# Seven-product steps for layers 2 and 3 of neighbouring pairs in a four-layer graph network

## The chip, the cores and the metric

The kernel runs on one core of a Trainium2 chip. The metric is the device time in microseconds, less being better. Arithmetic is in 32-bit floating point, with the masks of layer 1 in bfloat16. Engines are named as in the profile: PE (TensorE: matrix products), DVE (VectorE), ACT (ScalarE), POOL (GpSimd) and SP (SyncE). POOL and SP serve here as queues that issue DMAs.

## The reference, cut to what matters

x has 8 batches of 2048 nodes with 64 features, adj is a 2048x2048 matrix with rows normalised. There are four layers, each followed by `x = layernorm(x + layer(x))` over the 64 features:

```python
# layer 0: Chebyshev graph convolution, K = 3
As = [I, A, 2 A A - I]
out = einsum('bnki,nkio->bno', einsum('knm,bmc->bnkc', As, x), einsum('nd,dkio->nkio', embedding, weight)) + b
# layer 1: attention over all nodes; the mask is adj > 0.5
e = leaky_relu(s1[:, :, None] + s2[:, None, :]); att = softmax(where(mask, e, -9e15)); out = elu(att @ h)
# layer 2
out = (A + I) @ (x W^T + b) / deg
# layer 3, three steps; node 0 is set to a given value first
for _ in range(3):
    v = relu(concat[v, A @ v] W1^T + b1) W2^T + b2
```

So A, or A + I, multiplies the state of all batches twice in layer 0, once in layer 2 and three times in layer 3.

## The kernel before

**Pairs.** Two batches of 64 features make a pair of 128 columns, `NPAIR` = 4 pairs. A pair's state is a tile of [128 nodes, 16 blocks, 128 columns] (`SX[p]`, `SA`, `SB`, `SH`).

**Sweeps.** A product of the matrix with a pair is a `sweep` (L1128). It goes over four column blocks `c` of 512 nodes; in each, 16 matmuls of 128x128 by 128x512 add up in one of two PSUM banks (`acc_ring`). A sweep is 64 such multiplies. `multiply` (L400) splits one by columns into two halves that run side by side, where PE is in that form already. The 2 MiB of a column block come by DMA as eight tiles of 512 KB (`fetch`, L267, on SP's queue, `A_BUFS` = 6 buffers). With `plus`, tiles on the diagonal come from `a_plus_i`, a copy of A + I in HBM, which the first sweep makes. Layer 3's sweeps begin each block with a seed, one more multiply that adds the state times a weight to the bank (`SH_of[p]` by `w31v` in its first step, by `gv` = W2-W1 product later). Evictions (`z_evict`, `h_evict`) hand each finished block to `tails`, which makes the next operand from it: `layer2_tail` and `start_chunk` (embedding, layer norm, transposes), `u_chunk` (the block times W1's second half or `ge`, into `u_of(p, s)`), `last_chunk` (output and `store`).

**Order of the sweeps** (`sweeps`, L1400): layer 0 for all pairs, with layer 2 of pair 0 slipped in; layer 3 of pair 0 (three sweeps); layer 2 of pair 1; layer 3 of pair 1; layer 2 of pairs 2 and 3; at last layer 3 of pairs 2 and 3 together.

**Seven products.** `joint_layer3` (L1225) does that last part. Two pairs are taken as a matrix of two column halves, the nodes as two halves, so that a step is a product of 2x2 blocks, and it uses Strassen's method in Winograd's form: seven block products where eight would be plain. Their left factors are quarters of A and four sums of quarters, `sa` to `sd`, made beforehand in HBM by accumulating DMAs on POOL's queue (`sums_of_a`, L1191); their right factors are sums of u (`sums_of_u`, L1355, on DVE). A step has 7 x 2 x 8 = 112 multiplies and 8 seeds. Each product is done in two passes of 8 multiplies, one for each 512 columns, on the two banks; results are combined on DVE (`x_of`, `z_and_v`, `combine`), one is kept by a copy on ACT (`keep`).

**Layer 1** lies beside the sweeps. Its `scores` (L779) and `weights` (L857, L870) are instructions of [128, 2048] on DVE, its exponentials are ACT's, its products with the state (`po`, L884) PE's, its masks come on POOL's queue (L852, L766). Pair p leaves layer 1 when the token ("x2", p) is set in `finish`; layer 2 of the pair waits for that.

**Plan.** The order of all instructions is written at build time by a list scheduler (`Plan`). Each piece of work is a generator that yields the engine it wants and what it waits for. `Plan.go` always continues the one that can begin first by the planner's costs; a tie goes to the lower rank: 0 for `sums_of_u`, 1 for evictions, 3 for `tails`, 10 to 12 for the later pairs' `weights`, 1000 for the sweeps. `LAG`, `SLACK`, `HOLD` and `BACK` shift the planner's times for it. Some work has a due time: the rows of adj from 130 us on (`rows_of_adj`), the sums of A from 320 us on, one in 14 us.

Of the kernel before, what the change touches and what calls it, by code (L numbers as in the profile page):

```python
# [12 lines left out]
ALU = mybir.AluOpType  # L13
# [24 lines left out]
class Plan:  # L38
# [7 lines left out]
    SLACK = 0.3  # L46
# [5 lines left out]
    HOLD = 0.5  # L52
# [3 lines left out]
        ("add_terms", 0): -0.03,  # L56
        ("add_terms", 1): -0.11,
        ("add_terms", 2): -0.13,
        ("greatest", None): -1.14,
        ("out_of", None): 0.95,  # L60
        ("row_tile", None): -1.44,
        ("scores", 0): -1.14,
        ("start_chunk", None): -0.37,
        ("sums", None): 5.39,
# [111 lines left out]
def resnorm_d4_kernel(  # L176
# [251 lines left out]
    def weights_of_l23():  # L428
# [12 lines left out]

        yield "PE", [pp_ring, yt_ring]
# [28 lines left out]
    def rows_of_adj():  # L471


        for t in range(NT):
            yield "SP", [130.0 + 9.5 * t, bc_ring]
            an, k = bc_ring.take([P, 2, HALF], "an")
            an = an.rearrange("p a b -> p (a b)")
            nc.sync.dma_start(an, adj[t * P : (t + 1) * P, :])
            done = plan.dma("SP", 1024, bc_ring.t, 130.0 + 9.5 * t)
            plan.start(1, row_tile(t, an, k, done))  # L480
# [545 lines left out]
    def layer2_tail(p, c, z, kz, done):  # L1026
# [7 lines left out]
        yt_ring.give(kz, done)  # L1034
# [40 lines left out]
    def u_chunk(p, c, w, dst, bias, s, done):  # L1075

        room = {(0, 0): ["y1 used"], (0, 1): ["w0 used"], (2, 0): [("stored", 0, c)]}.get((p, s), [])
        yield "PE", [done, pp_ring, *room]
# [90 lines left out]
    def refill():  # L1169
        while ahead[0] < len(order_of_a) and a_ring.ready() < NEVER:  # L1170
            if spent[0] < AQ - 2 and ahead[0] > spent[0] + 3:
                break
            fetch(ahead[0])
            ahead[0] += 1
# [15 lines left out]

    def sums_of_a():  # L1191
        n = itertools.count()
        for m, a, b in (
# [5 lines left out]
            for x in (a, b):  # L1199
                for k, r in sum_tiles[m]:  # L1200
                    if x in QUARTER:
                        part = tile_of_adj(k + QUARTER[x][0], r + QUARTER[x][1])
                    else:
                        part = sum_tiles[x][k, r]
                    before = [("sum", m, k, r)] if x == b else []
                    if x not in QUARTER:
                        before.append(("sum", x, k, r, True))
                    yield "DMA", [320.0 + 14.0 * next(n), *before]
                    nc.gpsimd.dma_start(
                        sum_tiles[m][k, r], part, **({"accum_op": ALU.add} if x == b else {})  # L1210
                    )
# [3 lines left out]
    def order_of_joint():  # L1215
        for s in range(3):
            for m in ("sb", "a11", "sc", "sd", "a21", "a22", "sa"):
                for k in range(2):
                    for r in range(RQ):
                        if m in QUARTER:  # L1220
                            order_of_a.append((k + QUARTER[m][0], r + QUARTER[m][1], False))
                        else:
                            order_of_a.append((m, (k, r), False))

    def joint_layer3():  # L1225
        p, o = JOINT
# [4 lines left out]
        X, Z, V = buf[0:3]  # L1231
        T1, T3, T7 = (t.rearrange("p (t n) -> p t n", n=P) for t in buf[3:6])

        for s in range(3):
            up, uo = u_of(p, s), u_of(o, s)
            B11, B21, B12, B22 = up[:, 0:8], up[:, 8:16], uo[:, 0:8], uo[:, 8:16]
            T4, T6 = B21, B12
            plan.start(0, sums_of_u(s, B11, B21, B12, B22, T1, T3, T7))
            seed = gv if s else w31v
            half = lambda t, k: t[:, k * CW : (k + 1) * CW]  # L1240
            banks = {}

            def seeded(pair, c, pa, start):
                nc.tensor.matmul(  # L1244
                    pa,
                    lhsT=seed,
                    rhs=SH_of[pair][:, tiles(c), :],
                    start=start,
                    stop=False,
                    skip_group_check=True,  # L1250
                )
                plan.run("PE", mm(CW))

            def quarter(pa, B, need, start):
                for r in range(RQ):
                    n = next(used)
                    yield "PE", [("a", n), need(r // 2)]
                    at_, kt = a_tiles.pop(n)
                    for b in range(2):
                        nc.tensor.matmul(  # L1260
                            pa,
                            lhsT=B[:, 2 * r + b, :],
                            rhs=at_[:, b, :],
                            start=(start and r == 0 and b == 0),
                            stop=(r == RQ - 1 and b == 1),
                            skip_group_check=True,
                        )
                    done = plan.run("PE", mm(CW, 2), ("a", n), need(r // 2))
                    a_ring.give(kt, done)
                    spent[0] += 1  # L1270
                    refill()
                return done

            def keep(s, k, pa, done):
                yield "ACT", [done]
                nc.scalar.copy(half(X, k), pa)
                at["m5", s, k] = plan.run("ACT", act(CW), done)

            def x_of(s, k, pa, ka, done):
                yield "DVE", [done, ("m5", s, k)]  # L1280
                nc.vector.tensor_tensor(half(X, k), pa, half(X, k), ALU.subtract)
                at["x", s, k] = done = plan.run("DVE", dve(CW), done)
                acc_ring.give(ka, done)

            def z_and_v(s, k, pa, ka, done):
                yield "DVE", [done, ("x", s, k)]
                nc.vector.tensor_tensor(half(Z, k), half(X, k), pa, ALU.subtract)
                at["z", s, k] = done = plan.run("DVE", dve(CW), done)
                yield "PE", [done]
                seeded(p, 2 + k, pa, False)  # L1290
                done = plan.free["PE"] + plan.LAG
                yield "DVE", [done]
                nc.vector.tensor_tensor(half(V, k), pa, half(X, k), ALU.subtract)
                at["v", s, k] = done = plan.run("DVE", dve(CW), done)
                acc_ring.give(ka, done)

            def combine(s, k, what, pair, c, pa, ka, done):

                token = {"c11": "x", "c22": "z", "c21": "v"}[what]
                yield "DVE", [done, sq_ring, (token, s, k)]  # L1300
                tmp, kq = sq_ring.take([P, CW], "c")
                a = half({"x": X, "z": Z, "v": V}[token], k)
                nc.vector.tensor_tensor(
                    tmp, a, pa, ALU.subtract if what == "c21" else ALU.add
                )
                done = plan.run("DVE", dve(CW), done)
                if what == "c21":
                    at["c21", s, k] = done
                else:
                    acc_ring.give(ka, done)  # L1310
                yield from h_evict(pair, s, c, tmp, None, done)
                sq_ring.give(kq, plan.free["ACT"])

            u = lambda pair, side: lambda k: ("u", pair, s, 2 * side + k)
            t = lambda i: lambda k: ("t", s, i, k)
            for k in range(2):
                yield "PE", [acc_ring, u(o, 1)(0)]
                pa, ka = banks[k] = acc_ring.take([P, CW], "acc")
                done = yield from quarter(pa, B22, u(o, 1), True)
                plan.start(1, keep(s, k, pa, done))  # L1320
            for k in range(2):
                yield "PE", [("m5", s, k), ("h", o, s - 1, k)]
                pa, ka = banks[k]
                seeded(o, k, pa, False)
                done = yield from quarter(pa, T3, t(3), False)
                plan.start(1, h_evict(o, s, k, pa, ka, done))
            for k in range(2):
                yield "PE", [acc_ring, t(1)(0)]
                pa, ka = acc_ring.take([P, CW], "acc")
                done = yield from quarter(pa, T1, t(1), True)  # L1330
                plan.start(1, x_of(s, k, pa, ka, done))
            for k in range(2):
                yield "PE", [acc_ring, ("h", p, s - 1, 2 + k)]
                pa, ka = acc_ring.take([P, CW], "acc")
                done = yield from quarter(pa, B11, u(p, 0), True)
                plan.start(1, z_and_v(s, k, pa, ka, done))
            for k in range(2):
                yield "PE", [acc_ring, t(6)(0), ("h", o, s - 1, 2 + k)]
                pa, ka = acc_ring.take([P, CW], "acc")
# [140 lines left out]
```

## Time and profile before

| | us |
|---|---|
| median of three runs (lowest to highest) | 2085.89 (2083.27 to 2085.94) |
| profiled execution | 2081.43 |
| its span, from first to last instruction | 2079.5 |
| PE busy | 2042.8 (98%) |
| DVE busy | 1441.2 (69%) |
| ACT busy | 981.1 (47%) |
| POOL busy | 267.2 (13%) |

The mean granted clock of PE was 0.995 of full speed. The DMAs moved 531.18 MB. Landmarks of the span: the first sweep ends at 130 us; layer 1's weights run from 430 to 1600; the third step of layer 3 for pair 0 follows the eviction at 1187; layer 2 of pair 1 is evicted from 1290 to 1352; the third step of layer 3 for pair 1 follows the eviction at 1517; layer 2 of pair 2 is evicted from 1623 to 1672, that of pair 3 from 1688 to 1736; then come the three joint steps, the last store being issued at 2075. The sums of A are issued from 319 to 1211.

In the rows of the profile an instruction's duration is from its start to its modelled end; matmuls overlap, so the distance between starts tells PE's rate and the mean duration does not. A 32-bit multiply leaves two records.

### The profile page before, as it was taken

Reading aid. Unit: us, or ns where it says so; the run is one execution under the profiler, and the core shown is the slowest. Engines: PE = TensorE matmul, PEld = TensorE weight load, DVE = VectorE, ACT = ScalarE, POOL = GpSimd, SP = SyncE. Lnnn points to the kernel's source line nnn. Section 1 sums busy time; section 2 is a strip of 40 time slices with the busy share of each in tenths; the row PEclk is TensorE's granted clock in tenths of the full one; section 3 lists DMA queues with packets and bytes.
Section 4 is the critical chain, followed back from the end, with each engine's and each line's share of the span. In section 5 each row is a group of like instructions: output and inputs, shape, how many; then the busy total and the mean of one; then the engine's idle time right before and its main releaser. Section 6 shows DMA issues by size and latency. Waiting matters only on the chain.

```text
span 2079.5 us, 22115 instructions
## 1 busy us (share of the span) xinstructions
PE 2042.8 (98%) x7845; PEld 889.4 (43%) x7845; DVE 1441.2 (69%) x1847; ACT 981.1 (47%) x1791; POOL 267.2 (13%) x424
## 2 busy tenths in 40 slices
PE   8999999999999999999999999999999999999997
PEld 3444444444343443444344343443333455444444
DVE  2217566998899999979999979999798422121224
ACT  0015443378887567667766538427567211000002
POOL 2310001221111221021111111010000000000000
PEclk9999999999999999999999999999999999999999
DMA  9889867766546688688769999798787788888885
GB/s 299 290 311 330 306 202 242 279 177 158 141 147 223 164 278 300 221 273 253 251 224 282 287 313 328 255 331 280 243 278 233 256 262 265 266 265 271 263 285 186
DMA packets 223936, 531.18 MB, mean 255 GB/s; under 512 B 21506, under 2 KB 29826, under 8 KB 219458
## 3 DMA queue, kind: packets, MB, share of 16 engines
q1 hardware_dynamic: 170738, 360.73, 51.5%
q0 software_dynamic: 48864, 166.95, 26.4%
q10 hardware_dynamic: 4224, 2.10, 0.4%
q8 instruction: 62, 1.02, 0.2%
q14 instruction: 48, 0.39, 0.1%
HBM read 497.00 MB, written 64.16 MB: 270 GB/s over the span
## 4 chain that ended last, share of the span: by engine, by line
PE 86%; issue 5%; DMA 4%; DVE 3%; ACT 1%; SPq 0%; POOL 0%; POOLq 0%; DVEq 0%; ACTq 0%
PE acc L405 45%; PE yp L655 14%; PE acc L1260 10%; PE po L884 10%; DMA a<-in_adj_t 3%; PE ps_u L405 2%; DVE junk L779 1%; DVE terms L691 1%; PE acc L1244 1%; PE ps_emb L405 1%; PE pf L405 1%; ACT terms L679 1%; PE ps_sv L405 1%; ACT e L865 0%; DVE e L857 0%
## 5 line engine op out<-in xcount | busy, mean ns | idle before, releaser
L405 PE MATMUL acc<-a,SX 128*128 128x512 f32 (+1 forms) x1544 | 521.4, 596 | 7.9 <-DMA SX<-in_x 6.6
L405 PE MATMUL acc<-a,SB 128*128 128x512 f32 (+1 forms) x1000 | 354.7, 598 | 6.5 <-DMA a<-in_adj_t 5.8
L405 PEld LDWEIGHTS acc<-a,SX 128*128 128x128 f32 (+1 forms) x1544 | 196.5, 164 | 281.5 <-issue 270.3
L865 ACT ACTIVATE e<-e,sv 128x1024 f32<-128x1024 f32 x256 | 280.5, 1152 | 75.5 <-DVE e L857 75.1
L679 ACT ACTIVATE terms<-yp,emb_sb 128x128 f32<-128x128 f32 x896 | 242.4, 394 | 133.8 <-PE yp L655 133.4
L857 DVE TENSOR_TENSOR e<-s1b,mk 128x2048 f32<-128x2048 f32 x128 | 289.5, 2286 | 8.7 <-ACT e L865 4.7
L870 DVE TENSOR_TENSOR e<-e,mb 128x2048 f32<-128x2048 f32 x128 | 290.0, 2285 | 6.3 <-ACT e L865 6.1
L779 DVE CUSTOM_DVE_ANT_0 junk<-s2b,mr 128x2048 bf16<-128x2048 f32 x128 | 292.9, 2288 | 2.0
L873 ACT ACTIVATE e<-e 128x2048 f32<-128x2048 f32 x128 | 245.3, 1926 | 69.4 <-DVE e L870 69.1
L884 PE MATMUL po<-e,SX 128*64 128x512 f32 x1024 | 231.6, 595 | 0.0
L405 PEld LDWEIGHTS acc<-a,SB 128*128 128x128 f32 (+1 forms) x1000 | 130.5, 166 | 189.8 <-issue 176.4
L691 DVE TENSOR_TENSOR terms<-terms 128x512 f32<-128x512 f32 (+1 forms) x176 | 130.0, 739 | 27.6 <-ACT terms L679 23.4
L655 PE MATMUL yp<-SH,xgT 64*128 64x512 f32 x512 | 138.5, 618 | 5.6 <-ACT terms L679 4.8
L852 POOL DMA_DIRECT2D mk<-by_col x128 | 72.7, 587 | 526.4 <-DVE e L857 427.6
L655 PE MATMUL yp<-wk,xgT 64*128 64x512 f32 x512 | 132.0, 592 | 0.0
L884 PEld LDWEIGHTS po<-e,SX 128*64 128x64 f32 x1024 | 70.6, 137 | 143.3 <-issue 133.9
L655 PE MATMUL yp<-SH,y2T 64*128 64x512 f32 x512 | 131.2, 589 | 0.0
L405 PE MATMUL acc<-a,SA 128*128 128x512 f32 (+1 forms) x288 | 119.0, 597 | 2.7 <-DMA a<-in_adj_t 2.7
L1260 PE MATMUL acc<-a,t 128*128 128x512 f32 x192 | 85.4, 592 | 0.0
L655 PEld LDWEIGHTS yp<-SH,xgT 64*128 64x128 f32 x512 | 44.5, 187 | 79.2 <-issue 64.9
L655 PEld LDWEIGHTS yp<-wk,xgT 64*128 64x128 f32 x512 | 49.9, 188 | 60.8 <-issue 60.6
L655 PEld LDWEIGHTS yp<-SH,y2T 64*128 64x128 f32 x512 | 49.8, 188 | 60.7 <-issue 60.7
(239 smaller groups left out, 1784.8 us busy)
## 6 DMA issues: line engine op xcount, KB each, us to landing
a<-in_adj_t SPq DMA_DIRECT2D x520, 512.0 KB, 5.9
mr<-by_row POOLq DMA_DIRECT2D x64, 512.0 KB, 6.3
mk<-by_col POOLq DMA_DIRECT2D x128, 256.0 KB, 6.0
an<-in_adj SPq DMA_DIRECT2D x16, 1024.0 KB, 10.4
a<-a_plus_i SPq DMA_DIRECT2D x32, 512.0 KB, 4.4
a<-sb SPq DMA_DIRECT2D x24, 512.0 KB, 4.4
a<-sc SPq DMA_DIRECT2D x24, 512.0 KB, 4.4
a<-sd SPq DMA_DIRECT2D x24, 512.0 KB, 4.6
```

The lines of the kernel that those rows point to most:

```text
L405: nc.tensor.matmul(out[h], lhsT=lhsT[:, h], rhs=rhs, skip_group_check=True, **kw)
L655: nc.tensor.matmul(yp[:, e, :], lhsT=v[rows, cs], rhs=w[rows, hs], start=(k3 == 0), stop=(k3 == 2),)
L679: nc.scalar.activation(batches(terms[0][:, dd, :]), term, AF.Copy, scale=weight)
L691: nc.vector.tensor_tensor(a, a, b, ALU.add)
L779: nc.vector.tensor_tensor_reduce(out=junk, in0=s2b[e][0], in1=masks[t][0], scale=1.0, scalar=LOWEST, op0=ALU.add, op1=ALU.max, accum_out=m ...
L852: nc.gpsimd.dma_start(mk, by_col[jt // 2][:, jt % 2, h * HALF : (h + 1) * HALF])
L857: nc.vector.tensor_tensor(e, s1b[0], mk.unsqueeze(1).to_broadcast([P, 2, HALF]), ALU.add)
L865: nc.scalar.activation(e[:, i, :], e[:, i, :], AF.Prelu, bias=sv[:, 2 + i, jt : jt + 1], alpha=ALPHA)
L870: nc.vector.tensor_tensor(e, e, mb[0], ALU.add)
L873: nc.scalar.activation(e, e, AF.Exp)
L884: nc.tensor.matmul(po[i * C : (i + 1) * C, f, :], lhsT=SX[p][:, t, i * C : (i + 1) * C], rhs=e[:, i, f * CW : (f + 1) * CW], start=(t == 0 ...
L1260: nc.tensor.matmul(pa, lhsT=B[:, 2 * r + b, :], rhs=at_[:, b, :], start=(start and r == 0 and b == 0), stop=(r == RQ - 1 and b == 1), skip ...
```

## The change

The seven-product step is made a function of its own, `joint_step(p, sp, o, s, ...)`, which does step `sp` of pair p together with step `s` of layer 3 of pair o; with `sp` None it does layer 2 of pair p instead, without seeds for it, and its results go to `layer2_tail`. `joint_layer3` calls it three times as before. New is `joined(p)`, called for p = 1 and p = 2 in place of two sweeps: layer 3's third step of pair p-1 and layer 2 of pair p in one seven-product step. Its buffers are `wk1` and the two tiles of `xg_ring`, which layer 0 has left; two of its sums of u take the place of operands that are used up, so those sums wait (for `m5`, for `c22`).

As layer 2 multiplies by A + I, the shared sums and quarters are made of A + I, and layer 3 must use it too: `w31v` becomes W1's first half less its second. In `joint_step` the multiplies go through `multiply`, so that they can take the column form. The sums of A are due from 420 us on, one in 8 us, each as two DMAs of half the size; a tile of a sum isn't fetched before the plan has its sum. `u_chunk` of pair 1 waits for the whole of its joined step. The planner's `SLACK`, `HOLD`, `BACK` and the due times of the rows of adj are changed.

```diff
-    SLACK = 0.3
+    SLACK = 0.0
...
-    HOLD = 0.5
+    HOLD = 0.0
...
     BACK = {
-        ("add_terms", 0): -0.03,
-        ("add_terms", 1): -0.11,
-        ("add_terms", 2): -0.13,
-        ("greatest", None): -1.14,
-        ("out_of", None): 0.95,
-        ("row_tile", None): -1.44,
-        ("scores", 0): -1.14,
-        ("start_chunk", None): -0.37,
-        ("sums", None): 5.39,
+        ("h_evict", None): 0.64,
+        ("keep", None): -0.94,
+        ("layer1", None): -0.21,
+        ("mask_of_tile", None): 5.38,
+        ("tails", None): -0.13,
     }
...
+        nc.vector.tensor_tensor(w31v, w31v, w31e, ALU.subtract)
...
-            yield "SP", [130.0 + 9.5 * t, bc_ring]
+            yield "SP", [115.0 + 9.0 * t, bc_ring]
...
+        if s == 0 and p == 1 and p in JOINED:
+            room = [("joined", p)]
...
+            m, at_, _ = order_of_a[ahead[0]]
+            if isinstance(m, str) and ("sum", m, *at_, True) not in at:
+                break
...
+    SUMS = 420.0
...
-                        part = tile_of_adj(k + QUARTER[x][0], r + QUARTER[x][1])
+                        c, q = k + QUARTER[x][0], r + QUARTER[x][1]
+                        part = a_plus_i[q] if c == q // 2 else tile_of_adj(c, q)
...
-                    yield "DMA", [320.0 + 14.0 * next(n), *before]
-                    nc.gpsimd.dma_start(
-                        sum_tiles[m][k, r], part, **({"accum_op": ALU.add} if x == b else {})
-                    )
+                    yield "DMA", [SUMS + 8.0 * next(n), *before]
+                    for i in range(2):
+                        nc.gpsimd.dma_start(
+                            sum_tiles[m][k, r][:, i, :],
+                            part[:, i, :],
+                            **({"accum_op": ALU.add} if x == b else {}),
+                        )
...
+    def joint_step(p, sp, o, s, bufs, sums):
+
+        X, Z, V = bufs
+        up, uo = SX[p] if sp is None else u_of(p, sp), u_of(o, s)
+        B11, B21, B12, B22 = up[:, 0:8], up[:, 8:16], uo[:, 0:8], uo[:, 8:16]
+        T1, T3, T7, T4 = sums
+        T6 = B12
+        tag = (p, o, s)
...
+            yield "DVE", [done, ("x", tag, k)]
+            nc.vector.tensor_tensor(half(Z, k), half(X, k), pa, ALU.subtract)
+            at["z", tag, k] = done = plan.run("DVE", dve(CW), done)
+            if sp is not None:
                 yield "PE", [done]
                 seeded(p, 2 + k, pa, False)
                 done = plan.free["PE"] + plan.LAG
...
+            if pair == p and sp is None:
+                queue2.append(lambda: layer2_tail(p, c, tmp, kq, done, sq_ring))
+                at["q2", len(queue2)] = done
+                return
...
+        for k in range(2):
+            yield "PE", [
+                ("c21", tag, k),
+                t(4)(0),
+                *([("h", p, sp - 1, k)] if sp is not None else []),
+            ]
...
+    JOINED = (1, 2)
+    room_of_joined = []
+
+    def joined(p):
+        if not room_of_joined:
+            yield "PE", ["w0 used", ("x2", p)]
+            assert xg_ring.ready(2) < NEVER
+            for i in range(2):
+                t, _ = xg_ring.take([P, 2, CW], "ut")
+                room_of_joined.append(t.rearrange("p a n -> p (a n)"))
+        R1, R2 = room_of_joined
+        T3, T1 = (t.rearrange("p (t n) -> p t n", n=P) for t in (R1, R2))
+        B22 = u_of(p - 1, 2)[:, 8:16]
+        yield from joint_step(p, None, p - 1, 2, (wk1, R2, R1), (T1, T3, B22, T1))
+        at["joined", p] = 0.0
...
-            if p:
-                yield from sweep(layer2_product(p))
-            for s in range(3):
+            for s in range(2):
                 yield from sweep(layer3_product(p, s))
-        yield from sweep(layer2_product(NPAIR - 2))
+            if p + 1 in JOINED:
+                yield from joined(p + 1)
+            else:
+                yield from sweep(layer3_product(p, 2))
+                yield from sweep(layer2_product(p + 1))
```

The order of a joined step's products is that of a joint step: m5 and then the sum with T3 on the same banks (pair p-1's blocks 0 and 1), T1, B11, T6 (pair p-1's blocks 2 and 3), T7 (pair p's blocks 2 and 3) and T4 on T7's banks (pair p's blocks 0 and 1).

## The prediction

> **What bounds the kernel now.** I read the page's first two parts first: is there an engine with no time to spare, and where in the span.
>
> ```profile
> span 2079.5 us, 22115 instructions
> PE 2042.8 (98%) x7845; PEld 889.4 (43%) x7845; DVE 1441.2 (69%) x1847; ACT 981.1 (47%) x1791; POOL 267.2 (13%) x424
> ...
> PE   8999999999999999999999999999999999999997
> ...
> DVE  2217566998899999979999979999798422121224
> ```
>
> PE has 36.7 us of idle time in all, so work taken from PE is worth its full price unless something becomes late. The second row is the one to fear: from slice 8 to slice 31 (400 to 1620 us) DVE is nearly as full as PE, by layer 1; after that it is idle and PE works alone.
>
> The groups by shape price the work:
>
> ```profile
> L870 DVE TENSOR_TENSOR e<-e,mb 128x2048 f32<-128x2048 f32 x128 | 290.0, 2285 | 6.3 <-ACT e L865 6.1
> ...
> L1303 DVE TENSOR_TENSOR c<-u,acc 128x512 f32<-128x512 f32 x12 | 8.3, 688 | 40.0 <-PE acc L1260 40.0
> ```
>
> The chain of waits in order of time gives PE's true rate, from a stretch of one joint step where nothing interrupts:
>
> ```profile
> 1880.85 20.60 PE acc L1260 x48
> ```
>
> That is 0.429 us a record. One multiply of 128x128 by 128x512 leaves two records (four of half the price where it is split by columns), so it costs 0.858 us. The stage table shows that a joint step already runs without a gap (110.0 of 110 us busy), and how much room DVE has in the stages where the change puts new ones (columns: us, then busy us of PE, PEld, DVE):
>
> ```profile
> 1187.00:1355.00 168.00, 167.00 (x804) 73.23 (x801) 150.24 (x177) 90.45 (x115) 21.22 (x37) 1.00 0.88 297
> 1355.00:1517.00 162.00, 156.53 (x653) 63.15 (x653) 140.05 (x121) 78.19 (x75) 18.58 (x34) 0.98 0.83 287
> 1517.00:1672.00 155.00, 155.00 (x779) 64.34 (x776) 111.91 (x139) 86.24 (x109) 10.02 (x17) 1.00 0.77 251
> 1760.00:1870.00 110.00, 110.00 (x305) 52.66 (x304) 19.90 (x30) 6.67 (x11) 0.00 (x0) 1.00 0.81 268
> ```
>
> The timelines of DVE and ACT show the handover that matters. Pair 3 leaves layer 1 with its last normalisation, and PE turns to layer 2 of pair 3 when the last column block of pair 2 is evicted:
>
> ```profile
> 1639.84 0.69 DVE L557 TENSOR_TENSOR SX<-SX,ln_r 128x512 f32<-128x512 f32 x1
> ...
> 1672.00 0.59 ACT L995 COPY z<-acc 128x512 f32<-128x512 f32 x1 [2.85 <-PE acc L405]
> ```
>
> So pair 3 is ready at 1640.5 and needed at 1671.7: 31 us of slack today. Behind that point stand 2079.5 - 1671.7 = 408 us which the change doesn't touch.
>
> **PE: removed.** A pair of sweeps (layer 3's last step of pair p-1, layer 2 of pair p) is 2 x 64 multiplies and 4 seeds. A seven-product step is 7 x 2 x 8 = 112 multiplies and 4 seeds (layer 2 has none). Two steps save 2 x 16 x 0.858 = 27.5 us. The tails (u, embedding, transposes) are the same instructions. Multiplying by A + I takes no multiply away: the seeds stay, with W31v - W31e in place of W31v; the subtraction is one 128x128 DVE instruction at about 260 us, where DVE is 62% busy. Nothing.
>
> **DVE and ACT: added.** A step has 10 sums, 2 x, 2 z, 2 v and 6 combinations, 22 instructions of 0.69 us (the row of L1303): 15.1 us, 30.3 for both. ACT gains two copies of 0.585 a step and loses four, -1.2 us: nothing. Ranks 0 and 1 put the new DVE work ahead of layer 1's (rank 10 to 12), so it delays layer 1 except where layer 1 waits on its own chain. DVE idles 18 us in the first stage above and 22 in the second, mostly at 1200 to 1240 and 1490 to 1515. The first step starts near 1187; its sums and x fall at those places for some 4 us, 11 are delay. The second starts near 1505 and its first six sums fit the second gap; four or five instructions come after pair 3 has gone; 8 are delay. Pair 3 is ready at 1640.5 + 19 = about 1660. PE comes there at 1671.7 - 27.5 = 1644, plus its stalls below (8) = 1652. PE waits 8 us, of which it fills about half with the second step's own tails (embedding, transposes and u of pair 2: 4 x 2.2 us, today inside the sweeps). Price 4; ends 0 (all absorbed) and 1671 - 1644 = 27 (nothing absorbed and no filler).
>
> **New waits.** First, the way into a step: its first product needs u blocks 2 and 3 of the pair ahead, where a sweep took them in order and needed block 3 after a seed and 12 multiplies (11 us). From the eviction that starts at 1430.25 to its u on DVE takes 4.1 us, from 1186.99 5.7 us; now 4 multiplies (3.4 us) cover it. 0 to 2.3 a step; layer 1's products (6.9 us a piece, ready at both places) fill, so 1 for both.
>
> Second, the way out of the first step: pair 1's u goes to SB, which the step reads, so `u_chunk` waits for ("joined", 1); behind it in `tails` nothing else is due. The last block to leave is block 1, where it was block 3. Today's chain from that eviction to the product that needs its u:
>
> ```profile
> 1351.75 0.58 ACT L995 COPY z<-acc 128x512 f32<-128x512 f32 x1 [0.60 <-PE acc L405]
> ...
> 1367.55 3.70 PE L405 MATMUL acc<-a,SB 128*128 128x512 f32 x8 [0.67 <-ACT SB L393]
> ```
>
> 16 us, covered by 12 multiplies and tails, 0.67 us short. Then only 4 multiplies, a seed and about 6 us of tails cover: 16 - 3.4 - 0.9 - 6 = 6 short, less whatever layer 1 has ready. 0 to 11; I take 4. The second step has layer 2 of pair 3 behind it and needs no such cover. Inside a step each wait (m5 kept, x, z and v off a bank, c21 before its bank is used again) has one pass of 8 multiplies, 6.9 us, against at most two DVE instructions queued behind two of 2.29: 6.0. The new in-place waits (sum 7 behind m5, sum 4 behind c22) have two passes. 0.
>
> **DMA.** The sums of A move from 319-1212 us to about 420-930, each in two halves on POOL's queue. They are needed at 1187. What they pass there:
>
> ```profile
> 750.00:860.00 110.00, 108.69 (x479) 43.02 (x476) 106.47 (x114) 78.61 (x118) 16.75 (x29) 1.00 0.90 302
> ...
> L857 DVE TENSOR_TENSOR e<-s1b,mk 128x2048 f32<-128x2048 f32 x128 | 289.5, 2286 | 8.7 <-ACT e L865 4.7 <-PE po L884 1.5 <-DMA mk<-by_col 1.2
> ```
>
> Ten sums started in that stretch; at one per 8 us it would be 14, on queues 90% busy. What saturation costs is seen elsewhere:
>
> ```profile
> 1390.00:1400.00 10.00, 7.00 (x18) 2.95 (x18) 8.78 (x9) 0.00 (x0) 1.06 (x2) 0.99 1.02 391
> 1400.00:1410.00 10.00, 8.21 (x12) 2.37 (x12) 10.00 (x6) 6.56 (x6) 1.62 (x3) 0.67 1.04 392
> ```
>
> DMA share 1.02 to 1.04, four gaps of PE (4.8 us in all), and a granted clock of 0.67, worth 3.3 us more. One such place costs 8; I take 3, ends 0 and 8. From 930 to 1212 the queues are relieved, but PE loses nothing there now, so no gain.
>
> The Trainium skill, "TensorE: Matmul & The Clock Gate" (What's actually happening), has the clock halved only after a whole idle window of about 3.4 us. No gap in these two rows is longer than 2.4 us, so this rule would charge 4.8 us and not 8 for the place; the row decides. The skill also speaks against the halved transfers: "DMA: Bandwidth & Descriptors" (Rules for kernel authors) wants at least 1 MiB in one. The rows lean its way (256 KB of mk<-by_col land in 6.0 us, 512 KB of mr<-by_row in 6.3), but the sums have 250 us to spare.
>
> **The planner's numbers** (SLACK, HOLD, BACK, the rows' due times) reorder everything a little. No row prices them. A change between whole, row and column products costs PE about 0.1 us (0.96 instead of 0.86 to the next start at 240.03), and PE makes 164; twice as many would be +16, none -16. Two thirds of them lie in layer 0, whose work is the same; I take 0 and put 4 on either side.
>
> **Sum.** -27.5 + 4 + 1 + 4 + 3 = -15.5: span 2064. The profiled execution lasted 2081.4, 1.9 more than its span, the median of the runs 2085.9, 4.5 above it; on the median's footing about 2070. The sum charges each wait as if no other covered it; the way out, the DMA place and the wait for pair 3 overlap (PE that is late at the first waits less at the last), which takes 2 off: 2068.
>
> **Rivals.** *Layer 1 becomes the bound*: DVE absorbs nothing, pair 3 is ready at 1671, and the end stays where it is: 2078 to 2086. For it: DVE at 934 of 1020 us between 620 and 1640. Against: the gaps at 1200 and 1490 are chains that wait for PE, POOL and DMA, not for DVE. *Slower*: the crowded sums delay layer 1 itself. Its place is 420 to 930 us, where 48 masks (L857) are loaded on the queue that the sums now fill; each 0.5 us late is 24 us on the DVE chain, pair 3 is ready at 1684, the end is 12 us later, 2098. It decides from the point where layer 2 of pair 3 starts after 1672; it needs 12 us beyond the 19. Against: those loads hold DVE up for 1.2 us in all now. *It does not save*: if half of the 32 multiplies came back as seeds or idle banks, 2080.
>
> **Chances.** The forecast (2053 to 2078) 0.70, layer 1 as the bound 0.15, slower 0.11, no saving 0.04. The range goes from 27.5 and the planner's 4 off with no wait (2054.4; 2053 with a little for reading) to 2087, which takes in layer 1 as the bound. About 0.2%, 4 us, is what a measurement of this kernel can tell from no change: faster 0.80 (the forecast and most of the two cases near it), same 0.08, slower 0.12.
>
> **What would show it.** Right: 32 multiplies fewer (64 records of 128x512 in whole form); the two steps lasting some 100 us and more with fillers; layer 2 of pair 3 starting between 1645 and 1662, and 408 us from there to the end; DVE about 30 us busier, PE's idle time 40 to 50 us. Wrong: that start at 1670 or later, a PE gap before it longer than 10 us, a mean granted clock below 0.99, or L857 waiting for mk loads by more than 10 us.

## The result, and the profile after

The changed kernel takes 2072.8 us (median of six runs, 2070.24 to 2075.97) against 2085.91 before: a ratio of 0.9942, 95% interval 0.9932 to 0.9952. A second set of five runs gave 2071.55 and 0.9936 [0.9923, 0.9949]. The profiled execution took 2070.24 us, its span is 2068.5, 11.0 below the span of before.

The page's first two parts (span; busy time; DVE's row of the span in 40 slices, PE's being that of before):

```profile
span 2068.5 us, 22208 instructions
...
PE 2020.9 (98%) x7841; PEld 876.3 (42%) x7841; DVE 1469.3 (71%) x1893; ACT 978.0 (47%) x1786; POOL 301.7 (15%) x488
...
DVE  2225665998799999988999989999989832121224
```

DVE is 28.1 us busier; PE's idle time went from 36.7 to 47.6 us. The stage table, with the same columns as before (stage; length; busy of PE, PEld, DVE, ACT, POOL; granted clock; DMA share; GB/s):

```profile
1187.00:1355.00 168.00, 165.82 (x842) 71.87 (x839) 155.34 (x183) 100.41 (x120) 18.20 (x32) 1.00 0.77 270
1355.00:1517.00 162.00, 154.14 (x622) 63.46 (x622) 153.19 (x134) 76.41 (x75) 19.64 (x36) 1.00 0.86 302
1517.00:1661.00 144.00, 142.35 (x751) 58.17 (x748) 129.72 (x168) 87.64 (x108) 10.58 (x18) 1.00 0.73 237
```

The new steps run with small gaps, and DVE is at 92 to 95% in the first two stages, where it was at 86 to 89%. A joint step still runs without a gap (110.00 of 110 us busy from 1750 to 1860). The timelines at the handover (start, duration, instruction): the last normalisation of pair 3 in layer 1, the first multiplies of its layer 2, the first eviction of that sweep.

```profile
1660.76 0.69 DVE L555 TENSOR_TENSOR SX<-SX,ln_r 128x512 f32<-128x512 f32 x1
...
1661.79 7.03 PE L401 MATMUL acc<-a,SX 128*128 128x512 f32 x16
...
1677.05 0.58 ACT L993 COPY z<-acc 128x512 f32<-128x512 f32 x1 [4.57 <-PE acc L401]
```

Before, pair 3 was ready 31 us before it was needed. Now PE starts its sweep 0.3 us after it leaves layer 1. From that start to the end it takes 406.7 us (407.8 before).

**Lost time of PE.** To see where time went, I count PE's work: each record at its full rate (0.429 us for 512 columns, at least 0.11 for a short one, half of it where the multiply is split), all that started before a mark, and subtract it from the mark. What is left holds gaps, slow clock and changes of form. In all, PE's work is 1997.2 us before and 1969.7 after: 27.5 less, to the tenth. The lost time (up to 2000 us) grew from 70.9 to 87.6, so 16.7 us came back. It grew by 9.9 before 300 us, by 2.6 from there to 1200, by 1.2 in the first step (1200 to 1300), by 2.1 at the handover (1640 to 1700), by 0.9 elsewhere. Between two profiled executions of the changed kernel it differed by 2 us at 300.

The early loss is in stages that the two steps don't touch. PE's first instructions behind two gaps of the changed kernel, and rows of its table of windows:

```profile
141.43 8.67 PE L401 MATMUL acc<-a,SA 128*128 128x512 f32 x12 [3.14 <-DMA a<-in_adj_t]
...
261.56 1.12 PE L607 MATMUL ps_xg<-ident,SX 128*128 128x128 f32 x4 [3.62 <-ACT terms L677]
```

```profile
140.00:150.00 10.00, 8.57 (x12) 3.02 (x12) 0.00 (x0) 0.00 (x0) 1.80 (x3) 0.66 1.02 316
...
260.00:270.00 10.00, 8.44 (x17) 4.15 (x18) 8.87 (x24) 5.26 (x13) 2.50 (x4) 0.66 1.00 346
```

and of before:

```profile
140.00:150.00 10.00, 8.34 (x19) 3.63 (x20) 0.00 (x0) 0.58 (x1) 0.00 (x0) 1.00 1.05 384
...
250.00:260.00 10.00, 10.00 (x38) 3.98 (x35) 8.62 (x26) 6.78 (x17) 1.08 (x2) 0.86 0.86 350
```

The two gaps (3.14 us from 138 on for a tile of A, 3.62 from 258 on for ACT's `terms`) are each followed by a row of 10 us at a clock of 0.66, which costs 3.4 us. Between 120 and 300 PE is idle 3.7 us more than before (168.88 busy of 180, 172.53 before), and the mean clock is 0.96 in place of 0.99, worth 5.

### The profile page after: what moved, and what is told of

Read it like the earlier page. It is cut to its first block, busy times and chain, and to the rows that moved or that the text cites. A ratio compares the mean times of both kernels' runs of the same rounds, so it can differ in the third digit from the quotient of the medians.

```text
span 2068.5 us, 22208 instructions
## 1 busy us (share of the span) xinstructions
PE 2020.9 (98%) x7841; PEld 876.3 (42%) x7841; DVE 1469.3 (71%) x1893; ACT 978.0 (47%) x1786; POOL 301.7 (15%) x488
## 3 DMA queue, kind: packets, MB, share of 16 engines
q8 instruction: 62, 1.02, 0.2%
## 4 chain that ended last, share of the span: by engine, by line
PE 84%; issue 5%; DMA 5%; DVE 4%; ACT 1%; POOL 0%; SPq 0%; POOLq 0%; ACTq 0%; DVEq 0%
PE acc L401 53%; PE yp L653 15%; PE po L882 10%; DMA a<-in_adj_t 3%; DMA an<-in_adj 2%; PE ps_u L401 2%; DVE e L855 1%; PE ps_emb L401 1%; PE pf L401 1%; DVE e L868 1%; PE ps_sv L401 1%; PE ps_v L401 0%; PE ps_xg L607 0%; PE ps_vT L1064 0%; PE ps_xT L717 0%
## 5 line engine op out<-in xcount | busy, mean ns | idle before, releaser
L401 PE MATMUL acc<-a,SX 128*128 128x512 f32 (+1 forms) x1376 | 493.7, 597 | 10.0 <-DMA SX<-in_x 6.7
L401 PE MATMUL acc<-a,SB 128*128 128x512 f32 (+1 forms) x1096 | 378.2, 595 | 3.6 <-DMA a<-a_plus_i 2.3
L401 PEld LDWEIGHTS acc<-a,SX 128*128 128x128 f32 (+1 forms) x1376 | 189.6, 169 | 270.6 <-issue 252.9
L401 PEld LDWEIGHTS acc<-a,SB 128*128 128x128 f32 (+1 forms) x1096 | 141.1, 164 | 200.5 <-issue 191.6
L401 PE MATMUL acc<-a,SA 128*128 128x512 f32 (+1 forms) x396 | 181.7, 611 | 4.8 <-DMA a<-in_adj_t 4.8
L401 PEld LDWEIGHTS acc<-a,SA 128*128 128x128 f32 (+1 forms) x396 | 71.7, 192 | 97.2 <-issue 87.5
L401 PE MATMUL acc<-a,ut 128*64 128x512 f32 (+1 forms) x276 | 87.0, 594 | 2.0 <-DVE wk L1295 2.0
L1120 POOL DMA_DIRECT2D out<-SX x12 | 9.1, 755 | 467.2 <-DVE SX L555 428.3
```

The source lines that it names most:

```text
L401: nc.tensor.matmul(out[h], lhsT=lhsT[:, h], rhs=rhs, skip_group_check=True, **kw)
L1120: nc.gpsimd.dma_start(out[cols(c), p * P : (p + 1) * P].rearrange("(t p) n -> p t n", p=P), v)
```

## The experiments

The theories in the expectations: A, PE stays the bound and all it loses adds to the end; B, with the steps in, the exit of pair 3 from layer 1 sets the end; C, SLACK, HOLD and BACK are what loses PE's time early. "Exit" is the end of pair 3's last normalisation in layer 1.

| kernel | time, ratio [95%] | span | lost by 300 | by 1600 | by 1700 | exit |
|---|---|---|---|---|---|---|
| before | 2085.91 | 2079.5 | 25.6 | 69.4 | 69.8 | 1640.5 |
| changed | 2072.8, 0.9942 [0.9932, 0.9952] | 2068.5 | 35.5 | 83.6 | 86.5 | 1661.5 |
| e1_rows | 2090.33, 1.0029 [1.0016, 1.0041] | 2084.4 | 35.9 | 92.1 | 102.4 | 1675.8 |
| e2_plan | 2081.45, 0.998 [0.9967, 0.9994] | 2075.1 | 28.6 | 75.0 | 93.4 | 1678.4 |
| e3_plan_rows | 2069.11, 0.9926 [0.991, 0.9942] | 2067.3 | 26.9 | 74.1 | 85.7 | 1657.8 |
| e4_nojoin | 2095.01, 1.0043 [1.0027, 1.0058] | 2092.3 | 35.9 | 82.3 | 83.1 | 1633.6 |
| e5_extra | 2085.48, 0.9997 [0.9987, 1.0008] | 2081.6 | 28.2 | 84.8 | 95.1 | 1668.4 |
| e6_join2 | 2066.77, 0.991 [0.9888, 0.9931] | 2062.7 | 28.2 | 66.4 | 67.2 | 1638.4 |
| e7_join1 | 2075.81, 0.9945 [0.9928, 0.9963] | 2075.2 | 32.1 | 79.0 | 79.7 | 1650.0 |
| e8_pool | 2070.49, 0.9921 [0.9904, 0.9937] | 2067.1 | 28.2 | 84.8 | 85.2 | 1649.5 |
| e9_join2_after | 2096.6, 1.0054 [1.0041, 1.0067] | 2097.4 | 38.5 | 97.3 | 102.0 | 1636.1 |
| e10_back | 2113.23, 1.0138 [1.0124, 1.0151] | 2111.5 | 37.7 | 102.9 | 115.7 | 1650.2 |
| e11_slack | 2074.16, 0.9949 [0.9936, 0.9961] | 2072.7 | 34.2 | 76.7 | 77.5 | 1629.8 |
| e12_after | 2071.55, 0.9936 [0.9923, 0.9949] | 2069.8 | 37.7 | 85.3 | 87.8 | 1662.8 |

Ratios are to before, run on the same chip. Span, lost time and exit come from one profiled execution of each kernel. That of before took 2081.43 us, 4.5 less than the median of its runs; that of the changed kernel was 2.6 below its median, e6_join2's 2.3 below, e7_join1's 1.1 above. So differences of spans between kernels carry some 5 us of chance, and where they disagree with the ratios the ratios decide.

**The planner's numbers back, with both steps in.** e1_rows puts back only the due times of the rows of adj, e2_plan only SLACK, HOLD and BACK, e3_plan_rows all four.

```diff
-            yield "SP", [115.0 + 9.0 * t, bc_ring]
+            yield "SP", [130.0 + 9.5 * t, bc_ring]
```

> The changed kernel with the rows of adj due as before (130 us, one in 9.5 us); nothing else differs. PE's lost time (time less its multiplies at their full rate) stands 10 us above that of before already at 300 us, where the chain of waits goes through the row loads. Theory A, the loss is the row loads' and is on the path: lost time at 300 us falls from 35 to about 26, the span from 2068.5 to about 2059. Theory B, layer 1 sets the end and PE's early loss is covered: span within 3 us of 2068.5, layer 2 of pair 3 still starts near 1661. Theory C, the planner's SLACK, HOLD and BACK made the early loss: lost time at 300 us stays near 35.

> The changed kernel with SLACK, HOLD and BACK as before; the rows of adj stay at 115 us, one in 9 us. Theory A: lost time at 300 us stays near 35, span within 3 us of 2068.5. Theory C: lost time at 300 us falls to about 26, span about 2059. Theory B: span follows the time at which pair 3 leaves layer 1, whatever the early loss.

> The changed kernel with all four of the planner's numbers as before (SLACK, HOLD, BACK, rows of adj), so that only the seven-product steps and the sums of A differ from the kernel before. Theories A and C: lost time at 300 us near 26, span about 2059 (2079.5 - 27.5 + 7 for the crowded sums and the steps' waits). Theory B: layer 2 of pair 3 starts at 1656 or later and the span is 2064 to 2070.

The rows' due times don't cause the early loss (35.9), and alone they make the kernel slower, which no theory foresaw: exit 14 us later, and PE waits for it (6.1 us at once at 1670). SLACK, HOLD and BACK of before take most of the early loss away (28.6), as C has it, but the time doesn't follow. In e2_plan the exit is at 1678.4 and PE loses 18 us from 1640 to 1700. Its waits of PE from 1600 to 1720 us (total, times, longest):

```profile
PE acc L405 <- DVE SX L559: 6.1, 2, 5.0
PE po L886 <- ACT e L875: 5.2, 1, 5.2
```

Both are layer 1 of pair 3: its last normalisation and its exponentials. The end doesn't follow the exit one for one, though. PE began the sweep at 1661.65 here, with the blocks of pair 3 that were ready, and waited inside it: the exit is 16.9 us later than in the changed kernel, the span 6.6. e3_plan_rows is the clearest: by 1200 us it has lost 13.8 us less than the changed kernel, and its span is 1.2 us shorter (3.7 by the medians, with intervals that overlap). The rest goes at the handover, where PE comes early and stands still until pair 3 (exit 1657.8) and the tails of pair 2 are done; the timeline of PE, and the windows there:

```profile
1657.88 1.12 PE L1068 MATMUL ps_vT<-ident,SX 128*128 128x128 f32 x4 [4.92 <-DVE SX L559]
```

```profile
1650.00:1660.00 10.00, 3.96 (x19) 2.98 (x19) 8.41 (x23) 4.26 (x11) 0.00 (x0) 0.85 0.12 42
1660.00:1670.00 10.00, 10.00 (x26) 5.13 (x25) 0.00 (x0) 0.58 (x1) 0.00 (x0) 0.81 0.41 133
```

The gap brings a slow clock with it (0.85, 0.81: 3.4 us); 11.1 us are lost from 1640 to 1700 (0.4 before). So A fails with both steps in: what PE gains ahead of the handover it loses there, as B has it.

**No step, under the changed kernel's other parts.**

```diff
-    JOINED = (1, 2)
+    JOINED = ()
```

> The changed kernel with the two joined steps left out: four sweeps stand in their place, everything else (planner's numbers, sums of A + I, joint steps) stays. Theory A (the steps save 27.5 us less some 4 us of waits): span about 2092, pair 3 leaves layer 1 within 5 us of the 1661 of the changed kernel, so most of the 21 us that it is late there is not the steps' doing. Theory B (the steps' DVE work makes layer 1 late): pair 3 leaves layer 1 near 1642, span 2085 to 2088 as PE alone bounds it.

2095.01: the steps bring 22 us (23.8 of span), while the planner's numbers, A + I and the moved sums together cost some 9 (12.8 of span, 13.3 of lost time). The exit is at 1633.6 without the steps, 1661.5 with them. The span is theory A's (2092), as PE alone is the bound without the steps; the exit is B's, even earlier than its 1642.

**More work on DVE.** e3_plan_rows with two of the sums of u issued four times each, in all five seven-product steps, 60 instructions more (the expectation counts the two joined steps alone, 24):

```diff
-                    nc.vector.tensor_tensor(out[:, ks, :], a[:, ks, :], b[:, ks, :], op)
+                    for _ in range(4 if in_place and i in (3, 1) else 1):
+                        nc.vector.tensor_tensor(out[:, ks, :], a[:, ks, :], b[:, ks, :], op)
```

> As e3_plan_rows (span 2067.3, pair 3 out of layer 1 at 1657.8), but two of the joined steps' five sums of u are issued four times instead of once, with the order of all other instructions kept: 12 DVE instructions of 0.69 us more in a step, 16.5 us in all. Theory B (with the steps in, layer 1's exit of pair 3 sets the end, and all DVE work ahead of it counts): pair 3 leaves 10 to 16 us later, the span is 2077 to 2084, and PE's lost time grows only between 1640 and 1700. Theory A (PE is the bound, DVE has room): span within 3 us of 2067.

The exit moved by 10.6 us, the span by 14.3; the other 3.7 fall behind the exit, with the three joint steps. B's span is met, but not its place of the loss: PE has lost 10.7 us more than in e3_plan_rows by 1600 already, and from 1600 to 1700 no more than there (10.3, 11.6 there), as PE and the exit are late by the same amount. The loss begins with a gap at the first step that waits for layer 1's `mx` on DVE and brings a halved clock of 6.8 us (3.4 more):

```profile
1211.49 0.37 PE L834 MATMUL ps_rows<-ident,mx 128*16 128x128 f32 x1 [7.05 <-DVE mx L804]
```

DVE time before the handover costs PE time either way.

**One step at a time**, with the planner's numbers of before (e3_plan_rows has both):

```diff
-    JOINED = (1, 2)
+    JOINED = (2,)
```

> As e3_plan_rows, with the second joined step alone (pair 2's layer 2); layer 3's third step of pair 0 and layer 2 of pair 1 are sweeps again, 13.7 us of PE more. Theory B: pair 3 leaves layer 1 some 8 to 11 us earlier, near 1648, PE comes after that and waits for nothing, so that the lost time at 1700 stays under 80; span near 2070, 3 us above e3 and not 13.7. Theory A: span near 2081.

> As e3_plan_rows, with the first joined step alone (pair 1's layer 2); layer 3's third step of pair 1 and layer 2 of pair 2 are sweeps. Theory B: pair 3 leaves layer 1 near 1650, PE comes after it; span near 2070 and lost time at 1700 under 82. Theory A: span near 2081.

With the second step alone the exit is at 1638.4, 2 us earlier than before the change, and PE reaches layer 2 of pair 3 at 1654.0 without waiting. The window, DVE's exit and PE's start of the sweep in e6_join2:

```profile
1500.00:1661.00 161.00, 161.00 (x871) 65.31 (x868) 134.08 (x177) 89.39 (x110) 10.57 (x18) 1.00 0.77 249
```

```profile
1637.72 0.69 DVE L559 TENSOR_TENSOR SX<-SX,ln_r 128x512 f32<-128x512 f32 x1
...
1654.04 3.60 PE L405 MATMUL acc<-a,SX 128*128 128x512 f32 x8
```

161 us with no gap at all: the step saves its whole 13.7 us and costs PE nothing there (the kernel's span is 16.8 under that of before; the other 3 are lost time, 2 of it from 1300 to 1500, ahead of the step). Both theories expected more time, 2070 and 2081. The first step alone brings 4.3 us of span, but 11.5 by its ratio, between theory B's 2070 and A's 2081. No kernel without steps was run under the numbers of before, so what each step brings here includes what A + I and the moved sums cost. The first step delays the exit by 9.5 us, or by 19.4 with the second step in; the second delays it by 7.8 with the first in. With both, the exit lies at 1657.8, later than PE's arrival at 1654.0 with the second step alone, so the 13.7 us that the first step saves can't bring the sweep forward at all. e6_join2 has the lowest median of this study, some 5 to 6 us below the changed kernel (its interval just misses that of the changed kernel's first set of runs and just overlaps that of the second).

**Sums of u on POOL.** e3_plan_rows with four of the five sums of a step issued on POOL, again in all five steps, 40 instructions (the expectation counts 16):

```diff
+                if in_place and i != 7:
+                    yield "DMA", after(k)
+                    nc.gpsimd.tensor_tensor(out[:, ks, :], a[:, ks, :], b[:, ks, :], op)
+                    at["t", tag, i, k] = plan.run("DMA", 1.5, *after(k))
+                    continue
```

> As e3_plan_rows, with four of the five sums of u of the joined steps on POOL instead of DVE: 16 DVE instructions of 0.69 us fewer, 11 us in all; POOL is 15% busy. Theory B: pair 3 leaves layer 1 some 6 to 10 us earlier and the span falls by as much, to 2058 to 2062, unless POOL's reads hold DVE's or its queue holds the mask loads, in which case it is 2065 or more. Theory A: within 3 us of 2067.

The exit did come 8.3 us earlier (1649.5), and PE no longer waits at the handover. The time is the same, as theory A has it, but because PE lost 10.7 us more ahead of it, by 1600. From POOL's groups, the two dearest (busy, mean ns):

```profile
L1410 POOL TENSOR_TENSOR ut<-SB 128x512 f32<-128x512 f32 x4 | 13.0, 3250 | 24.4 <-DVE SB L1094 24.4
L1410 POOL TENSOR_TENSOR ut<-SX,SB 128x512 f32<-128x512 f32 x4 | 11.2, 2826 | 0.0
```

By its mean over each group POOL needs 1.26 to 3.25 us for what DVE does in 0.69. That PE's new gaps (3.5 us at 1349, 3.7 at 1544) come from these sums isn't shown: their rows name a normalisation and an eviction.

**The numbers once more, with only the second step**, where PE is the bound and a loss should show in full. e9_join2_after is the changed kernel with `JOINED = (2,)`; e10_back is e6_join2 with the changed BACK, e11_slack e6_join2 with `SLACK = 0.0` and `HOLD = 0.0`; e12_after is the changed kernel again.

> The changed kernel with all its planner's numbers, but only the second step joined (pair 2's layer 2 with pair 1's last step); layer 3's last step of pair 0 and layer 2 of pair 1 are two sweeps again. Theory A (every wait of PE adds to the end): the 10 us that PE loses by 300 us under these numbers come on top of the version with the numbers of before: 2066.8 + 10 = about 2077. Theory B (layer 1's exit of pair 3 sets the end wherever PE is early): with one step that exit lies near 1650 and PE, 10 us later than in the version with the numbers of before, still reaches it without waiting, so here B says 2077 too, and lost time of about 78 us in all (68 there). If instead the early loss is covered with one step as it was with two, about 2067.

> Only the second step joined, the planner's SLACK, HOLD and rows of adj of before, but BACK of the changed kernel. It asks which of the numbers loses PE's 10 us by 300 us. If BACK does: about 35 us lost by 300 us of span (28 with BACK of before), and the time about 7 to 10 us above 2066.8, as PE never waits for pair 3 with one step (theory A). If SLACK and HOLD do: 28 us lost by 300, and 2065 to 2069. Theory B, layer 1's exit as the bound, expects no change as long as the exit of pair 3 stays near 1650: 2067.

> Only the second step joined, the rows of adj and BACK of before, but SLACK and HOLD at 0.0 as in the changed kernel. The counterpart of the last one. If SLACK and HOLD lose PE's 10 us by 300 us: 35 us lost there and about 2074 to 2077 in all (theory A: it adds up). If BACK does: 28 us lost by 300 and 2065 to 2069. Theory B: 2067 in either case, as long as pair 3 leaves layer 1 near 1650.

> The changed kernel itself once more, on the chip of the three others, so that the versions with one step are compared with it directly: 2070 to 2076 by either theory, with the same gaps of PE (3.14 us at 138 us, 3.62 at 258).

e11_slack is A's case: 9.8 us more lost by 2000 us than in e6_join2, a span 10.0 longer (7.4 by the medians). SLACK and HOLD at zero lose 6 us by 300 us, and BACK alone 9.5, so each of them loses time early; all of the numbers together lose 10.3 (e9_join2_after). The other two were missed by 20 and 36 us by every theory, and BACK is common to both. Of the 34.8 us that e9_join2_after has lost more than e6_join2 by 1700, 10.3 are lost by 300, 8.3 from there to 1500, and 15.7 in the second step, from 1500 to 1640. On PE a bank of the step is full at 1565, the other at 1580; on ACT their two evictions come at 1604.60, after the last exponential of layer 1, where e6_join2 evicts them at 1545 and 1557, each at once when the bank is full:

```profile
1600.57 1.91 ACT L871 ACTIVATE e<-e 128x2048 f32<-128x2048 f32 x1 [0.15 <-DVE e L868]
1602.78 1.91 ACT L871 ACTIVATE e<-e 128x2048 f32<-128x2048 f32 x1 [0.29 <-DVE e L868]
1604.60 1.25 ACT L1001 ACTIVATE SH<-acc,b31n 128x512 f32<-128x512 f32 x2
```

Until then PE has no free bank for the step; it is left with layer 1's products, each of which waits for its exponential:

```profile
1593.59 4.99 PE L882 MATMUL po<-e,SX 128*64 128x512 f32 x16 [4.81 <-ACT e L871]
1602.54 5.35 PE L882 MATMUL po<-e,SX 128*64 128x512 f32 x16 [3.96 <-ACT e L871]
```

```profile
1580.00:1590.00 10.00, 6.98 (x32) 1.76 (x28) 9.89 (x6) 9.23 (x8) 1.60 (x3) 1.00 0.56 177
1590.00:1600.00 10.00, 4.99 (x16) 1.39 (x16) 9.95 (x5) 9.24 (x8) 0.00 (x0) 0.83 0.13 54
```

e10_back has the same two evictions at 1618.69 and five such waits, 16.4 us. It had lost 25 us more than e6_join2 by 1200 already, 9.5 of them by 300; between 300 and 1200 PE waited once for an exponential for 6.0 us and three times for tiles of A, 5.4 in all, and what else that loss holds stays open. BACK alone is shown to be enough for it all, as e10_back differs from e6_join2 in nothing else; e11_slack, with the old BACK, doesn't have these waits. That its entry ("h_evict", None): 0.64 does it, by letting every ready exponential go ahead of a ready eviction as long as ACT has one, is argued from the code and wasn't tried alone. The changed kernel escapes it: its evictions in that step start at 1541 and 1553. Why, stays open.

e12_after meets its time, not its gaps: a tile of A was waited for for 5.1 us and `terms` for 4.3, where the first profile had 3.14 and 3.62.

## Why the prediction was right, and where it was off

**PE: removed, 27.5.** Measured 27.5. The gain is in the work, and no cost came back as seeds. (Half of it lost, the case of the last rival, would have been 2082 by the sum, not 2080.)

**DVE added, exit at 1660, 408 us behind it.** DVE 28.1 us busier (30.3 predicted), exit at 1661.5, 406.7 us behind the start of the sweep. The sum of 19 us of delay held (21.0; 17.3 with the old numbers), but not its split into 11 and 8: with the old numbers the first step alone delays the exit by 9.5 and the second alone by nothing (2.1 earlier than before); it is the two together that do it.

**The handover, 4.** PE had 1.65 us of gaps there, both for pair 2's tails and not for the exit itself, and lost 2.4 (0.4 before). But the sum had half of the wait filled by tails drawn ahead, so that 4 of 408 us would be saved behind it; 1.1 were. As the exit sets the start, that term is 3 us of the miss.

**The way in, 1; inside a step, 0; the way out, 4.** Inside the first step DVE's `x_of` came late once (1.96 us at 1248, behind two weights instructions), where I had written 0. The way out:

```profile
1359.69 0.63 PE L1064 MATMUL ps_vT<-ident,SX 128*128 128x128 f32 x4 [1.63 <-DVE SX L555]
1361.00 1.16 PE L401 MATMUL ps_u<-w31e,SH 128*128 128x128 f32 x8 [0.68 <-ACT SH L389]
1362.83 1.98 PE L401 MATMUL acc<-a,SB 128*128 128x512 f32 x4 [0.68 <-ACT SB L389]
```

3.0 us in three gaps, by the chain that was named. Little of it shows in the end: from 1300 to 1640 PE lost 12.1 us before and 12.9 after, as the crowded place at 1390 to 1410 cost 8.1 before (4.8 us of gaps, 3.3 of clock) and its like at 1415 to 1434 only 4.9 of gaps after.

**DMA, 3.** Right in size, but that the halved sums are the cause isn't shown. From 300 to 1200 us 2.6 more were lost than before, with the DMA share at 1.02 from 750 to 860. But e3_plan_rows has the same halves of sums and lost 2.6 less than before in that stretch; the share was 0.94 there (0.90 before), so the crowding itself goes with the planner's numbers, and what the 2.6 us are stays open. The rival that ends slower had no footing: `weights` waited for its masks for 2.3 us in all (groups by shape; idle time of DVE before them, and what ended it).

```profile
L855 DVE TENSOR_TENSOR e<-s1b,mk 128x2048 f32<-128x2048 f32 x128 | 290.2, 2285 | 5.9 <-PE po L882 2.9 <-DMA mk<-by_col 2.3 <-issue 0.5
```

The Trainium skill's rule of at least 1 MiB in one DMA ("DMA: Bandwidth & Descriptors", Rules for kernel authors) speaks against the halves, but no run here shows what they cost.

**The planner's numbers, 0 with 4 on either side: the term that was mis-sized.** They cost 9.9 us of PE by 300, and putting them back took 8.6 of it away (e3_plan_rows, 26.9). I had priced only the changes of form (174 now, 164 before, a microsecond); what they moved was when PE waits for `terms` and a tile of A, and the two longest of these waits brought a slow clock.

**The overlap, 2.** Also too small. The waits don't add, because the exit sets the start of the last 407 us: 13.8 us of lost time given back in e3_plan_rows brought 1.2 of span. This is why a miss of 10 in one term moved the end little: with that term at its predicted zero (e3_plan_rows) the span was 2067.3, not 2064, as the handover then cost 11, within its ends of 0 and 27. That the forecast of 2068 came within 5 us of 2072.8 is partly luck: the largest cost was put at nothing, and most of it went uncharged only because PE, had it come earlier, would have waited for pair 3 instead. The first rival, layer 1 as the bound, had the right mechanism at the wrong price: DVE absorbed about a third of the 30 us. In e1_rows its forecast is there in full, exit at 1675.8 and span 2084.4.

## What to carry to other kernels

Before work is taken from the full engine, read when the next stage's other input is ready: slack of 31 us was spent by 28 us of saved work and 21 us of delay that the saving itself put on the second engine, and with equal planner's numbers half of the change was worth at least about as much as the whole (16.8 us of span against 12.2; 18.8 against 15.4 by the ratios, whose intervals overlap). A gain that can't be had twice should be taken where it delays the other engine least, here in the second step. Planner weights tuned for one order are not safe for another: the changed numbers cost some 4 us with both steps in, which is hardly clear of noise, and 30 with one.

## What the runs showed of the hardware

A short gap of PE cost up to as much again in clock. The granted clock went to 0.50, for 3.4 us or a multiple of it; 6.8 us at 0.50 are the rows at 0.66 above. Whether it did so hung on where the gap lay. Rows of the changed kernel, ahead of and behind the gap's end at 141.43, and of e8_pool around a gap of 3.66 us that ended at 1548.04:

```profile
137.40:140.80 3.40, 0.89 (x3) 0.06 (x1) 1.76 (x5) 0.00 (x0) 1.71 (x4) 1.00 1.03 382
140.80:147.60 6.80, 6.17 (x7) 2.35 (x8) 0.00 (x0) 0.00 (x0) 1.00 (x2) 0.50 1.00 295
...
1543.00:1546.40 3.40, 1.38 (x8) 0.21 (x4) 3.33 (x5) 1.52 (x2) 0.00 (x0) 1.00 1.08 364
1546.40:1549.80 3.40, 1.76 (x20) 1.21 (x22) 3.37 (x5) 2.73 (x5) 0.54 (x1) 1.00 0.35 142
```

In each of the 14 traces of the table the slow stretches begin on a grid of 3.413 us. Between 90 and 2050 us PE was idle for 2.04 us or more in 59 steps of these grids, and the step behind each of them had the clock at 0.50. No step with less than 1.7 us idle began a slow stretch; in between it went either way. So the longer gap of e8_pool, shared by two steps (2.0 and 1.6 us idle), cost nothing in clock, and the shorter one at 138 (2.5 us in one step) cost 3.4. The place at 1400 before the change is of the same kind: four gaps of at most 2.36 us, 2.4 of them within the 3.4 us ahead of 1399.7, gave 0.67 from 1400 to 1410; six of at most 1.8 us at 1415 to 1434 after the change, 4.9 us together, left the clock at 1.00. The Trainium skill ("TensorE: Matmul & The Clock Gate", What's actually happening) has the clock halved after a whole idle window of about 3.4 us; the length of the window agrees, but here some 2 us of idle time in one were enough.
